# Three changes of order in a fused two-layer transformer on one core: choice of experts, first queries of layer 1, sums of x's quarters

## The chip, the core and the metric

One core of one Trainium2 chip runs the whole program in one launch. The core has five engines that work side by side and meet through semaphores: TensorE (PE, matrix products; its weight loads are listed as PEld), VectorE (DVE), ScalarE (ACT), GpSimd (POOL) and SyncE (SP, which here only issues DMAs). The metric is the device time of one execution in microseconds, lower is better; times are medians of runs. Verdicts on a pair of kernels come with a 95% interval.

## The reference

Eight batches of 512 tokens of 512 features go through two post-norm layers. Layer 0 is causal attention with 16 heads of 32 and a mixture of 8 experts, of which each token takes the best two. Layer 1 is grouped-query attention behind a root-mean-square norm, and a gated network with integer weights. Cut to what the change touches:

```python
x = L0_attn_x                                     # (8, 512, 512)
x = _layernorm(x + _L0_attn_ref(x, ...))          # causal, 16 heads of 32
x = _layernorm(x + _L0_ffn_ref(x, ...))           # 8 experts, top 2
x = _layernorm(x + _L1_attn_ref(x, ...))          # 8 query heads, 2 key/value heads of 64
x = _layernorm(x + _L1_ffn_ref(x, ...))           # silu(gate) * up, hidden 1408

# in _L0_attn_ref
v = (x @ WV_w.T + WV_b).reshape(b, s, NH, HD).transpose(0, 2, 1, 3)
# in _L0_ffn_ref
probs = jax.nn.softmax(router_logits, axis=-1)
routing_weights, selected = jax.lax.top_k(probs, TOP_K)
routing_weights = routing_weights / routing_weights.sum(-1, keepdims=True)
# in _L1_attn_ref
q = (h @ Wq.T).reshape(b, s, H, dh)
k = (h @ Wk.T).reshape(b, s, G, dh)
v = (h @ Wv.T).reshape(b, s, G, dh)
```

## The kernel before

**The stages.** Layer 0's attention runs for the eight batches one after another (from the start to about 670 us), and the choice of experts for each batch runs among the attention of the batches behind it. Then come the experts' tiles (to about 1048 us): rows of 128 tokens are gathered for one expert each, pass its two products, and are written to DRAM. Then layer 1's attention (to about 1580 us) and its integer network (to the end at 2083 us).

**Layer 0's attention.** `attention0` works on one batch `b`, four groups of four heads `g`, and three units `u` of key tiles (`UNITS`). A slot is a pair (g, u). In each slot it issues the scores on PE, their exponential on ACT (L1573) and the causal select on POOL (L1583); then the thunks that `plan` has put into `todo` for that slot; then the product with the values of the unit before; then the thunks of `late`. At u = 1 `normalise` closes the group of heads before: a product sums the rows (rs), ACT and DVE build the inverse (L78 to L81), and DVE multiplies it into the output (L1634). `normed[0]` holds that last instruction. POOL then adds the inverse to a guard's total (L1110). For each unit DVE adds the exponentials up (L1620, "sum of p" below). Products that end in the shared pool of two PSUM banks (`mm`: queries, keys, projections, value products, logits, ranks) need a bank that its last reader has emptied.

**Sums of x's quarters.** From batch 1 on, the value projection is computed with seven products instead of eight (`seven`, order 1, 6, 2, 5, 3, 7, 4). Four of them read sums of quarters of x^T, not x^T itself. `seven_of_rows` (L798, the subtraction at L806) makes these four sums on DVE, 128x512 elements each, from the next batch's x^T, which SP loads while the present batch runs. `plan` puts two of them into `late` of slot (0, 2) and two into slot (1, 0) (for the first batch (2, 1) and (2, 2)). `seven` empties its banks with L1437 on DVE and L1440 on ACT.

**Choice of experts.** `Router.choose(b)` makes from the logits the two best experts of each token, with small DVE instructions on 128x32 and 128x4 elements (L534 to L565). `both` and `earlier` count the tokens that former tiles gave to each expert. `dispatch(b)` multiplies these by two constant matrices (ps_rank, with L564's `earlier` as the second product's input), and so gets each token's place in its expert's list. In a batch b > 1, `choose(b - 2)` stands in slot (0, 0), and slot (1, 0) issues, in this order, the projection of the batch before (ps_o, emptied by L1495 into x), the first of the seven products, and `dispatch(b - 2)`.

**What sets the order.** In `attention0` PE's order is as written at the start and the end (`in_order`); the other engines are ordered by the framework's scheduler, which places instructions by when it expects their inputs. `tc.issue_after(i)` keeps what is issued inside it behind instruction i. From the experts' tiles on, and in layer 1's attention, PE, DVE, ACT and POOL all run in the order written.

**The seam to layer 1.** The first batch of layer 1's attention is prepared beside the last tiles of the experts: `first_pieces` gives a list of steps, of which one is taken after every second tile: fetches, adds, the norm, blocks of a transpose, two empty steps, and then the key, value and first query products, each copied out of PSUM by ACT (L1853, L1862, L1871). Behind the last tile comes a branch that skips three rare tiles (`rare`, L1070, the branch at L1074), in which all engines take part; then layer 1's attention loads ACT's table for the exponential (L1929) and starts with the scores, which read the key and the query.

Of the kernel before, what the change touches and what calls it, by code (L numbers as in the profile page):

```python
# [14 lines left out]
ALU = mybir.AluOpType  # L15
# [421 lines left out]
class Router:  # L437
# [80 lines left out]
    def choose(self, b, parts, ps, columns):  # L518

        nc, small = self.nc, self.small  # L520
        here = slice(NT * b, NT * (b + 1))

        def bc(a):
            return a[:, :, None].to_broadcast([P, NT, E])

        for t in range(NT):
            matmul_by_columns(nc, ps[:, t, :], parts[:, ts(t, P)], self.gather, columns=columns)
        pr = small.tile([P, NT, E], F32, name="pr")
        tmp = small.tile([P, NT, E], F32, name="tmp")
        top = small.tile([P, NT], F32, name="top")  # L530
        second = small.tile([P, NT], F32, name="second")
        red = small.tile([P, NT], F32, name="red")
        total = small.tile([P, NT], F32, name="total")
        nc.vector.tensor_reduce(red, ps, AX.X, ALU.max)  # L534
        nc.vector.tensor_tensor(tmp, ps, bc(red), ALU.subtract)
        nc.scalar.activation(tmp, tmp, AF.Exp)
        nc.vector.tensor_reduce(red, tmp, AX.X, ALU.add)
        nc.vector.reciprocal(red, red)
        nc.vector.tensor_tensor(pr, tmp, bc(red), ALU.mult)

        def first_of_largest(values, largest, one_hot):
            nc.vector.tensor_reduce(largest, values, AX.X, ALU.max)
            nc.vector.tensor_tensor(tmp, values, bc(largest), ALU.is_equal)
            nc.vector.tensor_tensor(tmp, tmp, self.iota, ALU.mult)
            nc.vector.tensor_reduce(red, tmp, AX.X, ALU.min)
            nc.vector.tensor_tensor(one_hot, self.iota, bc(red), ALU.is_equal)

        first_of_largest(pr, top, self.hots[:, 0, here, :])

        rest = small.tile([P, NT, E], F32, name="rest")  # L550
        nc.vector.scalar_tensor_tensor(rest, self.hots[:, 0, here, :], -2.0, pr, ALU.mult, ALU.add)
        first_of_largest(rest, second, self.hots[:, 1, here, :])
        nc.vector.tensor_tensor(total, top, second, ALU.add)
        nc.vector.reciprocal(total, total)
        nc.vector.tensor_tensor(self.weights[:, 0, here], top, total, ALU.mult)
        nc.vector.tensor_tensor(self.weights[:, 1, here], second, total, ALU.mult)


        self.both = small.tile([P, NT, E], F32, name="both")
        nc.vector.tensor_tensor(self.both, self.hots[:, 0, here, :], self.hots[:, 1, here, :], ALU.add)  # L560
        self.earlier = small.tile([P, NT, E], F32, name="earlier")
        nc.vector.tensor_copy(self.earlier[:, 0, :], self.carry)
        for t in range(1, NT):
            nc.vector.tensor_tensor(self.earlier[:, t, :], self.earlier[:, t - 1, :], self.both[:, t - 1, :], ALU.add)  # L564
        nc.vector.tensor_tensor(self.carry, self.earlier[:, NT - 1, :], self.both[:, NT - 1, :], ALU.add)  # L565

    def dispatch(self, b, ps, columns):

# [765 lines left out]
def attention0(env, guard, keep, routes, experts, dram, p_mm, tiles_ctx):  # L1334
# [4 lines left out]
    tc, nc, ins, xs, vec = env.tc, env.nc, env.ins, env.xs, env.vec  # L1339
# [4 lines left out]
    with ExitStack() as phase:  # L1344
# [77 lines left out]
        def row_sums(b):  # L1422
            return seven_of_rows(nc, xts[b], t_x)

        def seven(b, n):
            x_of, _ = row_sums(b)
            room = v_rooms[b % 2]
            ps = mm([P, 2, 256], f"ps_{n}of7")
            for s in range(2):
                for k in range(2):  # L1430
                    matmul_by_columns(nc, ps[:, s, :], x_of[n][:, k, ts(s, P)], v_of[n][:, k, :], start=k == 0, stop=k == 1)

            def block(i, j):
                return room[:, 2 * j : 2 * (j + 1), 256 * i : 256 * (i + 1)]

            def add(out, a):
                nc.vector.tensor_tensor(out, ps, a, ALU.add)  # L1437

            if n == 1:
                nc.scalar.copy(block(0, 0), ps)  # L1440
            elif n == 6:
                add(block(1, 0), block(0, 0))
            elif n == 2:
                add(block(0, 0), block(0, 0))
            elif n == 5:
                add(block(1, 1), block(1, 0))
            elif n == 3:
                add(block(0, 1), block(1, 1))
            elif n == 7:
                add(block(1, 1), block(1, 1))  # L1450
                add(block(1, 0), block(1, 0))
            else:
                add(block(1, 0), block(1, 0))
# [186 lines left out]
        merging, inverses, normed = {}, [], [None]  # L1640
# [6 lines left out]
        def plan(b):  # L1647

            todo, late = ({(g, u): [] for g in range(ND) for u in range(len(UNITS))} for _ in range(2))
            if b == 0:  # L1650
                for slot, places in (((0, 0), (0, 1)), ((0, 1), (3,)), ((0, 2), (2,))):
                    todo[slot] += [lambda t=t: value(b, t) for t in places]
                late[1, 0] += [lambda: v_sums(False), spread_bias]
                todo[1, 1].append(out_of_bias)
                late[1, 1].append(lambda: v_sums(True))
            else:
                todo[0, 0].append(lambda: seven(b, ORDER[-1]))
            pb, last = b - 1, b == NB - 1
            by_dma = 0 <= pb < by_blocks
            for g in range(ND):  # L1660
                nb, ng = (b, g + 1) if g + 1 < ND else (b + 1, 0)
                if nb < NB:
                    todo[g, 0 if by_dma and ng == 0 else 1].append(lambda nb=nb, ng=ng: query(nb, ng))
                    todo[g, 1 if by_dma and ng == 0 else 2].append(lambda nb=nb, ng=ng: key(nb, ng))
            if b:
                places = ((1, 0), (1, 1), (1, 2), (2, 0)) if by_dma else ((1, 0), (1, 0), (1, 1), (1, 1) if last else (1, 2))
                for t, slot in enumerate(places):
                    todo[slot].append(lambda t=t: project(pb, t))
                if by_dma:
                    todo[2, 1].append(lambda: blocks(pb))  # L1670
                else:
                    for c in range(ND):
                        at = todo[2, 1] if last and c >= 2 else (late if last else todo)[2, 0]
                        at.insert(c % 2 if at is todo[2, 1] else len(at), lambda c=c: turn(pb, c))
                todo[(3, 2) if by_dma else (2, 1)].append(lambda: score(pb))
                if not by_dma:
                    todo[(3, 0) if last else (2, 2)].append(lambda: choose(pb))
            if b == 0:
                todo[1, 0].append(lambda: router.merge_lora(mm([P, ND, E], "ps_wr")))
            if b + 1 < NB:  # L1680
                for slot, last_sums in (((0, 2), False), ((1, 0), True)) if b else (((2, 1), False), ((2, 2), True)):
                    late[slot].append(lambda last_sums=last_sums: row_sums(b + 1)[1](last_sums))
                for n, slot in zip(ORDER, ((1, 0), (2, 0), (2, 1), (2, 2), (3, 0), (3, 2)) if b else
                                   ((3, 0), (3, 0), (3, 1), (3, 1), (3, 2), (3, 2))):
                    todo[slot].append(lambda n=n: seven(b + 1, n))
            if b > 1:
                todo[0, 0].append(lambda: choose(b - 2, mm=aside))
                todo[1, 0].append(lambda: dispatch(b - 2))
                if last:
                    todo[1, 2].append(lambda: behind(enter(one_hot(b - 2, range(NT))), normed[0]))  # L1690
                else:
                    todo[1, 2].append(lambda: enter(one_hot(b - 2, range(NT))))
            if last:
                todo[1, 2].append(soon)
                todo[2, 2].append(first_rows)
                late[3, 1].append(first_turned)
                todo[3, 2] += [begin, lambda: dispatch(b - 1)]
            return todo, late
# [96 lines left out]
class Attention1:  # L1795
# [83 lines left out]
    def first_pieces(self):  # L1879
# [7 lines left out]
        def blocks(tiles):  # L1887
            for t in tiles:
# [1 line left out]

        return ([lambda t=t: fetch(t) for t in range(NT)] + [lambda t=t: do["add"](t) for t in range(NT)]
                + [do["deviations"], do["norm"], lambda: blocks((0, 1)), lambda: blocks((2, 3)), lambda: None, lambda: None]
                + [do["key"], do["value"], lambda: do["query"](0)])

    def scale(self, c):

# [554 lines left out]
```

## Time and profile before

| | us |
|---|---|
| median of 3 runs | 2086.05 |
| lowest and highest run | 2085.02, 2086.63 |
| the profiled execution, its own time | 2084.99 |
| its span, first to last instruction | 2083.3 |
| granted clock of PE, mean | 0.998 |

Busy time of PE by stage, from the view by windows (columns: us of the window, then busy us and number of instructions of each engine, the granted clock, the share of the DMA engines and GB/s):

```profile
50.00:150.00 100.00, 100.00 (x1346) 36.73 (x1338) 58.14 (x68) 40.27 (x48) 40.28 (x35) 1.00 0.13 44
...
250.00:350.00 100.00, 100.00 (x1488) 38.29 (x1484) 74.84 (x143) 44.65 (x59) 47.05 (x44) 1.00 0.40 121
...
450.00:550.00 100.00, 98.99 (x1400) 36.74 (x1392) 71.25 (x135) 41.16 (x54) 44.56 (x39) 1.00 0.37 120
...
1000.00:1100.00 100.00, 97.40 (x484) 41.44 (x485) 40.93 (x47) 33.39 (x54) 29.10 (x24) 1.00 0.34 101
```

The second column is PE: it is busy nearly without a break in each window. The fourth is DVE, the sixth POOL. A row of the waits, as the prediction shows them, reads: who waited on which line, for whom, us in total, how often, and the longest. A row of a timeline: start, length, engine, line, operation, what it writes and reads, and in brackets the idle time of the engine before it and who ended it.

### The profile page before, as it was taken

The page shows a single profiled execution, that of the slowest core. Times are in us where ns is not written, and L with a number is a line of the kernel's source. Part 1 is how long each engine was busy: PE and PEld are TensorE (multiplying, and loading weights), DVE is VectorE, ACT ScalarE, POOL GpSimd, SP SyncE. Part 2 cuts the span into 40 slices and gives each one's busy share as a digit, 9 for nine tenths or more (in the row PEclk, how much of TensorE's full clock was granted, in tenths as well). Part 3 has the DMA queues.
Part 4 walks back from the last instruction along what each step waited for, and adds up shares of the span by engine and source line. Part 5 has one row for each costly group of instructions (what it writes and reads, how often), then busy time and mean ns, then how long its engine had stood idle before and what let it go on. Part 6 is the DMA issues. An engine that isn't in the chain of part 4 may idle for free. (4 is left out here: it accounts for less than half of the span.)

```text
span 2083.3 us, 37551 instructions
## 1 busy us (share of the span) xinstructions
PE 2058.4 (99%) x15778; PEld 1069.4 (51%) x15778; DVE 1264.3 (61%) x2047; ACT 645.3 (31%) x916; POOL 510.7 (25%) x509
## 2 busy tenths in 40 slices
PE   9999999999999999999999999999999999999998
PEld 2333333333334677764433333333335888888886
DVE  3667687686777533233158889887868644455444
ACT  2444434344344111111143333333332322222222
POOL 1344444444435121221052231232101000000000
PEclk9999999999999999999999999999999999999999
DMA  6023424415334488876432332223102311111000
GB/s 208 22 83 123 143 81 145 150 63 173 107 139 177 153 222 256 245 228 187 129 102 62 112 122 71 77 96 102 41 1 71 101 41 61 61 61 61 21 21 22
DMA packets 193059, 226.10 MB, mean 109 GB/s; under 512 B 73818, under 2 KB 139610, under 8 KB 189298
## 3 DMA queue, kind: packets, MB, share of 16 engines
q1 hardware_dynamic: 180240, 185.44, 28.3%
q0 software_dynamic: 10560, 34.61, 5.7%
q10 hardware_dynamic: 2082, 3.56, 0.6%
q8 instruction: 127, 2.08, 0.4%
q14 instruction: 50, 0.41, 0.1%
HBM read 138.88 MB, written 84.69 MB: 107 GB/s over the span
## 5 line engine op out<-in xcount | busy, mean ns | idle before, releaser
L1573 ACT ACTIVATE p<-sc 128x2048 f32<-128x2048 f32 (+1 forms) x96 | 152.4, 1587 | 175.8 <-PE sc L67 175.8
L1262 DVE SCALAR_TENSOR_TENSOR hT<-ps_u,vec,sg 128x512 f32<-128x512 f32 x88 | 65.6, 745 | 189.4 <-PE ps_u L1257 189.1
L1583 POOL TENSOR_SCALAR_AFFINE_SELECT p<-p 128x512 f32<-128x512 f32 x128 | 97.2, 771 | 307.6 <-ACT p L1573 302.0
L1273 PE MATMUL ps_f<-ffn_w,h_half 128*128 128x512 f32 x664 | 167.6, 393 | 2.8 <-DVE h_half L1268 2.0
L990 PE MATMUL ps_gu<-xrT,experts 128*128 128x256 f32 x736 | 166.6, 379 | 0.0
L1110 POOL TENSOR_TENSOR g_total<-g_total,r_inv 128x512 f32<-128x512 f32 x64 | 83.7, 1308 | 316.2 <-DVE r_inv L2007 270.6
L1620 DVE TENSOR_TENSOR p<-p 128x1536 f32<-128x1536 f32 (+2 forms) x96 | 147.8, 1539 | 17.7 <-POOL x L1593 10.0
L990 PEld LDWEIGHTS ps_gu<-xrT,experts 128*128 128x128 f32 x736 | 139.3, 190 | 35.9 <-issue 19.3
L1977 ACT ACTIVATE p<-sc 128x1024 f32<-128x1024 f32 x128 | 124.2, 1022 | 100.5 <-PE sc L67 99.2
L2007 DVE RECIPROCAL r_inv<-r_inv 128x512 f32<-128x512 f32 x32 | 107.1, 3347 | 71.6 <-ACT r_inv L1107 71.6
L1273 PEld LDWEIGHTS ps_f<-ffn_w,h_half 128*128 128x128 f32 x664 | 122.9, 188 | 34.5 <-DVE h_half L1268 7.4
L1257 PE MATMUL ps_g<-x_high,ffn_w 128*128 128x512 f32 x352 | 137.2, 390 | 0.0
L1257 PE MATMUL ps_g<-x_low,ffn_w 128*128 128x512 f32 x352 | 137.0, 389 | 0.0
L1257 PE MATMUL ps_u<-x_low,ffn_w 128*128 128x512 f32 x352 | 136.9, 389 | 0.0
L1257 PE MATMUL ps_u<-x_high,ffn_w 128*128 128x512 f32 x352 | 136.9, 389 | 0.0
L67 PE MATMUL ps_q<-experts 128*32 128x512 f32 x1024 | 120.1, 603 | 6.1 <-DMA experts<-in_xT 4.3
L67 PE MATMUL sc<-qT,kT 64*64 64x512 f32 x1024 | 124.7, 602 | 1.2 <-ACT qT L1871 0.9
L1260 ACT ACTIVATE sg<-ps_g,vec 128x512 f32<-128x512 f32 x88 | 60.6, 689 | 195.6 <-PE ps_g L1257 195.6
L1996 PE MATMUL av<-p,v 128*64 128x512 f32 x512 | 120.8, 593 | 0.0
L202 POOL TENSOR_SCALAR rstd<-mv 128x4 f32<-128x4 f32 x15 | 3.9, 262 | 461.9 <-DVE mv L201 461.9
L67 PE MATMUL ps_k<-experts 128*32 128x512 f32 x1024 | 116.4, 595 | 0.0
L67 PE MATMUL ps_o<-attn_out,aoT 128*64 128x512 f32 x512 | 116.4, 598 | 0.0
(310 smaller groups left out, 3419.2 us busy)
## 6 DMA issues: line engine op xcount, KB each, us to landing
results<-y SPq DMA_DIRECT2D x68, 256.0 KB, 2.6
pair<-xrT SPq DMA_DIRECT2D x30, 512.0 KB, 3.3
xrT<-pair SPq DMA_DIRECT2D x120, 128.0 KB, 3.9
turned<-turned SPq DMA_DIRECT2D x56, 256.0 KB, 4.1
merged<-merged SPq DMA_DIRECT2D x48, 256.0 KB, 2.4
experts<-merged SPq DMA_DIRECT2D x8, 1536.0 KB, 6.6
x<-in_x SPq DMA_DIRECT2D x8, 1024.0 KB, 8.4
merged<-in_gate_up SPq DMA_DIRECT2D x32, 256.0 KB, 3.9
```

What stands on the lines that cost most here:

```text
L67: nc.tensor.matmul(out[m], lhsT=lhsT[:, m], rhs=rhs, start=start, stop=stop)
L990: nc.tensor.matmul(ps[:, j, :], lhsT=w, rhs=xT[:, c, :], start=c == 0, stop=c == ND - 1)
L1110: self.nc.gpsimd.tensor_tensor(self.total, self.total, r_inv, ALU.add)
L1257: nc.tensor.matmul(ps, lhsT=w[:, ts(dc, P)], rhs=x[:, dc, :], start=(dc, i) == (0, 0), stop=(dc, i) == (ND - 1, 1))
L1262: nc.vector.scalar_tensor_tensor(hT, u, vec[:, V_SU + c : V_SU + c + 1], sg, ALU.mult, ALU.mult)
L1273: self.nc.tensor.matmul(os[t], lhsT=h[:, ts(t, P)], rhs=self.weights(2 * NHID + c), start=(c, i) == (0, 0), stop=(c, i) == (NHID - 1, 1))
L1573: nc.scalar.activation(p, sc[:, :, :width], AF.Exp, scale=scale)
L1583: select = nc.gpsimd.affine_select(out=first, in_=first, pattern=[[0, 4], [1, P]], compare_op=ALU.is_ge, fill=0.0, base=0, channel_multipl ...
L1620: nc.vector.tensor_tensor(total[:, :, P * kt :], total[:, :, P * kt :], p[:, :, at : at + w], ALU.add)
L1977: nc.scalar.activation(p, sc, AF.Exp, scale=scale)
L1996: nc.tensor.matmul(st["av"][HD * j : HD * (j + 1), :], lhsT=st["v"][:, kt, HD * j : HD * (j + 1)], rhs=p[:, j, :], start=kt == 0, stop=kt ...
L2007: nc.vector.reciprocal(r_inv, r_inv)
```

## The change

Three edits, each of order alone; what is computed stays the same.

1. In `Router.choose`, the four instructions that turn the two best probabilities into weights (sum, reciprocal, two products) are written behind the sums over former tiles, no longer ahead of them.
2. In `Attention1.first_pieces`, the first query product and its copy take the step before the value product and its copy, and the value product the last step.
3. In `attention0`, the sums of x's quarters for the next batch are issued behind `normed[0]`, the instruction that finished the last normalised tile when the sums are issued. The slots stay.

```diff
@@ Router.choose
         first_of_largest(rest, second, self.hots[:, 1, here, :])
-        nc.vector.tensor_tensor(total, top, second, ALU.add)
-        nc.vector.reciprocal(total, total)
-        nc.vector.tensor_tensor(self.weights[:, 0, here], top, total, ALU.mult)
-        nc.vector.tensor_tensor(self.weights[:, 1, here], second, total, ALU.mult)
-
-
         self.both = small.tile([P, NT, E], F32, name="both")
...
         nc.vector.tensor_tensor(self.carry, self.earlier[:, NT - 1, :], self.both[:, NT - 1, :], ALU.add)
+        nc.vector.tensor_tensor(total, top, second, ALU.add)
+        nc.vector.reciprocal(total, total)
+        nc.vector.tensor_tensor(self.weights[:, 0, here], top, total, ALU.mult)
+        nc.vector.tensor_tensor(self.weights[:, 1, here], second, total, ALU.mult)
@@ attention0
         def row_sums(b):
             return seven_of_rows(nc, xts[b], t_x)
+
+        def sums_of_rows(b, last):
+            with tc.issue_after(normed[0].ins):
+                row_sums(b)[1](last)
@@ attention0, plan
                 for slot, last_sums in (((0, 2), False), ((1, 0), True)) if b else (((2, 1), False), ((2, 2), True)):
-                    late[slot].append(lambda last_sums=last_sums: row_sums(b + 1)[1](last_sums))
+                    late[slot].append(lambda last_sums=last_sums: sums_of_rows(b + 1, last_sums))
@@ Attention1.first_pieces
-                + [do["key"], do["value"], lambda: do["query"](0)])
+                + [do["key"], lambda: do["query"](0), do["value"]])
```

In the built program this moves the following. On PE, the first query product (4 instructions) and the value product (16) change places, and the sixteenth value product stands behind the branch. On ACT, the two copies change places. On DVE, the four sums of each of the batches 1 to 6 leave the places where they stood (two ahead of a sum of p, one on either side of the fourth product's emptying) and stand behind L1634, three of them ahead of a sum of p and one after it, in front of L1495; the first batch's four move likewise. POOL and SP keep their order, and the instructions of `choose` keep theirs.

## The prediction

> **What bounds the kernel now.** I read the page first, then the waits of PE over the whole span, the waits of DVE while layer 0's attention runs (100 to 650 us), the form of the one line that the third edit moves, and the timeline of one batch and of the seam between the expert tiles and layer 1's attention.
>
> ```profile
> PE 2058.4 (99%) x15778; PEld 1069.4 (51%) x15778; DVE 1264.3 (61%) x2047; ACT 645.3 (31%) x916; POOL 510.7 (25%) x509
> ```
>
> PE is busy for 2058.4 of 2083.3 us, and the granted clock is 9 tenths or more in every slice. No edit changes a product, so the change can only win back waits of PE, or add some. The waits of PE that bear on the three edits:
>
> ```profile
> engine line waited for: us in total, times, longest us
> ...
> PE ps_q L67 <- DVE experts L1437: 1.4, 2, 1.0
> ...
> PE sc L67 <- ACT qT L1871: 0.9, 1, 0.9
> ...
> PE ps_rank L67 <- DVE earlier L564: 0.7, 1, 0.7
> ```
>
> These three rows are all the change aims at: 3.0 us, or 0.14% of the span. A measurement of this kernel can tell about 0.2%, 4.2 us, from no change. The other engine's view is far larger, and misleads:
>
> ```profile
> DVE experts L806 <- DMA experts<-in_xT: 31.1, 5, 7.2
> ...
> L806 DVE TENSOR_TENSOR experts<-experts x20: 675/692/1802, 171.3 to 511.1; 128x512 f32<-128x512 f32 x20
> ```
>
> L806 holds the sums of x's quarters. Five times DVE stood in front of them until the next batch's x had landed, 31.1 us in all. PE did not stand with it: of that, only what reaches PE counts, and it is the 1.4 us above (the bank of a value product, emptied late by L1437, that the next query product wants).
>
> **First edit, weights behind the sums over former tiles: nothing.** It aims at the 0.7 us of the last row, where the ranks' product waits for L564. But DVE isn't under a written order there. In the built program the small instructions of the choice stand on DVE in the same order before and after, in all eight batches: the scheduler had interleaved them already (in the trace L555 and L556 run between steps of the second choice). Count, durations and waits are the same. This is the case in which the change doesn't do what it says, and for this part it is certain. Cost 0; if the order did change, the bound is 0.7 us gained.
>
> **Second edit, query ahead of value: 0.8 us gained.** At the seam the timeline says:
>
> ```profile
> 1045.66 1.28 ACT L1929 ACT_TABLE_LOAD   x1 [0.45 <-ACTq L1074]
> ...
> 1048.12 0.20 ACT L1929 ACTIVATE p_none<-neg_half 128x1 f32<-128x1 f32 x1 [1.17 <-PEq L1074]
> ...
> 1048.22 0.57 ACT L1871 COPY qT<-ps_q 128x512 f32<-128x512 f32 x1
> ...
> 1048.84 0.21 PEld L67 LDWEIGHTS sc<-qT,kT 64*64 64x64 f32 x8 [1.69 <-ACT qT L1871]
> ```
>
> The query product is the last before the branch that skips the rare tiles. Its copy is queued on ACT behind the table load and an empty exponential that itself waits for PE's side of the branch. Only then may the scores start, at 1048.84. With the query first, its copy falls where the value's copy stood (1036.48, beside expert tiles), and the scores need nothing of ACT. In its place the value's copy goes behind the table load; the first reader of the values (L1996) comes after two pairs of scores and another query product, at 1056.5. The products take as long either way (3.60 us for the query, 3.73 for the values). In the built program one of the 16 value products falls behind the branch (3.73/16 = 0.23 us), ahead of the scores. The score's wait was 0.9 us by the row; its sequencer work behind the branch is done by about 1048.4, so 0.46 us is the floor of the gain. On top, the last product before the branch is a short one (0.27 against 0.59 us), which lets the branch go 0.3 to 0.5 us earlier, less the 0.23. I take 0.8, with ends at 0.4 and 1.0.
>
> The Trainium skill speaks against this step (ScalarE: Activation LUTs, What ACT_TABLE_LOAD costs): a switch of tables costs the load of 1283 ns and a drain of 1380 ns. The trace agrees on the load (1.28), and by the row ACT is held until 1048.12 by the branch. By the rule it would be held to 1045.66 + 2.66 = 1048.32 whatever the branch does; the value's copy would then end by 1049.1 (estimate: 0.20 + 0.57 behind it). The first exponential can't start before the first scores, at about 1049.2 (1050.05 less 0.8). Row and rule give the same sum here, with 0.1 us to spare.
>
> **Third edit, sums behind a normalised tile: 1.4 us gained, 2.3 us lost.** The four sums of a batch leave their places (two before the sums of p, two inside the choice) and stand behind the product of L1634, three before the next sum of p and one after. Six batches have them so (the first batch's four move too, with much room: nothing). Their first reader, the product ps_6of, loads at 303.7 us in the batch shown below, some 25 us on. In the batch at 250 us:
>
> ```profile
> 252.87 1.42 DVE L806 TENSOR_TENSOR experts<-experts 128x512 f32<-128x512 f32 x2 [5.83 <-DMA experts<-in_xT]
> ...
> 254.20 2.96 DVE L1620 TENSOR_TENSOR p<-p 128x1536 f32<-128x1536 f32 x2
> ...
> 262.13 1.80 DVE L806 TENSOR_TENSOR experts<-experts 128x512 f32<-128x512 f32 x1
> ...
> 275.55 0.69 DVE L1634 TENSOR_TENSOR aoT<-av,r_inv 128x512 f32<-128x512 f32 x1
> 275.67 1.28 POOL L1110 TENSOR_TENSOR g_total<-g_total,r_inv 128x512 f32<-128x512 f32 x1 [4.36 <-DVE r_inv L81]
> ...
> 276.16 1.87 DVE L1620 TENSOR_TENSOR p<-p 128x1024 f32<-128x1024 f32 x1
> ```
>
> Gain: without the wait and the two sums, the sum of p at 254.20 starts at 251.1, when its select on POOL ends; without the other two (1.80 + 0.68) the choice ends about 3.5 us earlier. The next sum of p can then start when its select ends, at 268.72 instead of 271.64, and L1634 ends at about 273.4 instead of 276.24: 2.8 us earlier. L1437 empties its bank 2 to 3 us earlier, more than the longest wait of 1.0, so both waits of PE's row go: 1.4 us.
>
> Cost: what is late next is the emptying of the projection's bank, x<-ps_o of L1495. The ranks' product reuses that bank. The same timeline has L1495 end at 277.95 + 0.68 = 278.63 and the first weight load of ps_rank at 279.13: a margin of 0.50 us, and 0.44 to 0.57 in the other four such batches (five batches have ranks and sums both). Now L1634, three sums, the sum of p, one sum and L1495 stand in a row. Bare, four sums cost 4 x 0.69 = 2.76, against 2.8 gained: L1495 ends when it did. But POOL's g_total and two merges (1.28, then 3.51 for two from 276.90) follow the same r_inv, start 2.8 us earlier too, and run beside the three sums.
>
> Here the Trainium skill's rule (SBUF — State Buffer, Who interferes with whom) weighs most: a DVE instruction with two SBUF inputs and a GpSimd instruction that reads SBUF exclude each other, and whichever starts first holds the shared port for its whole length. The sums have two SBUF inputs. The row shows the case: the sum at 262.13, just behind a merge's start, took 1.80 instead of 0.69, 1.11 us lost. By the row alone, 5 of 20 sums were hit, one in four: 0.28 us a sum, about 1.1 a batch as before, no change, and the margin holds: cost 0. By the rule, each of the three sums meets a POOL instruction: 3 x 1.11 = 3.3. The sum of p behind them is freed of its own such wait (1.87 against about 1.22, halfway between the 0.69 of 512 columns and the 1.75 of 1536): 0.65 back. That leaves 2.7 late, less the margin 0.5: 2.2 us a batch, 11 us in five. I take about half of the port waits, 1.6, since the first sum overlaps g_total only in part and the last may come between: 1.6 - 0.65 - 0.5 = 0.45 a batch, 2.3 us in five.
>
> **Sum.** -0.8 - 1.4 + 2.3 = +0.1 us on the profiled execution, whose own time was 2084.99 us (span 2083.3). The median of the runs, 2086.05, lies 1.06 above it, so I put the changed kernel at 2086.2.
>
> **Rivals.**
> - *The ranks' product becomes the new wait.* Place: ps_rank in five batches; price up to 2.2 us each. From (4.2 + 2.2)/5 = 1.3 us a batch it decides. At full price: 2086.05 - 2.2 + 11 = 2094.9. For it: the rule, the 1.80 row, the thin margin. Against: DVE gains 2.8 us before it, and POOL's order may leave gaps. 0.14.
> - *Clean gain.* No port waits reach PE: -2.2, so 2083.8, which still counts as no change. To pass 0.2%, the other DVE waits of PE in this stretch (ps_x1T 0.7, ps_q on x1T 0.3, ps_rank 0.7) must go too, and a little more: 2086.05 - 2.2 - 1.7 = 2082.1 or less. Their order isn't touched. 0.08.
> - *The sums' wait never reached PE*, and the two ps_q waits stay: with the seam alone 2085.2. Part of no change.
>
> No change holds 0.78. The range 2083.3 to 2090.5 runs from a little under the clean gain (2083.8) to a stall of 1.3 us a batch (2090.3).
>
> **What would show it.** Right: DVE's 31.1 us before L806 gone; ps_q's wait on L1437 gone; the scores at the seam start without a wait for ACT; ps_rank waits for x of L1495 in five batches, each under 1 us; sums of 1.1 to 1.8 us beside g_total and the merges. Wrong: ps_rank waits of over 1.3 us, or a PE wait that isn't named here.

## The result, and the profile after

| | before | after |
|---|---|---|
| median of 20 runs each, us | 2085.85 | 2089.05 |
| lowest and highest run | 2084.63, 2086.83 | 2088.06, 2091.31 |
| the profiled execution, its own time | 2084.99 | 2091.31 |
| its span | 2083.3 | 2089.6 |

The ratio is 1.0016, with an interval of 1.0009 to 1.0023: 3.2 us slower, which is within 0.2% and still not nothing. The profiled execution of after is 2.26 us above its median, so its trace holds more than the 3.2 us that have to be explained.

The line of busy times shows no more work on PE than before, and DVE busier by 10.7 us in as many instructions:

```profile
PE 2059.9 (99%) x15778; PEld 1069.3 (51%) x15778; DVE 1275.0 (61%) x2047; ACT 647.2 (31%) x916; POOL 507.7 (24%) x509
```

The waits of PE over the whole span of after (us in total, times, longest):

```profile
PE ps_rank L67 <- DVE x L1497: 4.0, 5, 0.8
PE sc L67 <- ACT qT L1873: 2.9, 1, 2.9
...
PE ps_rank L67 <- DVE earlier L558: 0.7, 1, 0.7
```

The two waits of ps_q for L1437 (L1439 now) are gone. Five waits of the ranks' product for the projection's bank have come (L1497 is the old L1495), and one of 2.9 us in front of scores of layer 1. The last row, which the first edit was to shorten, is unchanged.

The waits of DVE from 100 to 650 us in front of that sum of p, before and after:

```profile
DVE p L1620 <- POOL x L1593: 10.0, 2, 5.3
...
DVE p L1622 <- POOL x L1595: 37.0, 7, 5.3
```

The 31.1 us in front of the sums of quarters have not turned into work done sooner: DVE now stands 37.0 us, not 10.0, in front of the next sum of p, until POOL's add behind the select has ended (L1595; in the batch below the select ends at 251.95, the add at 253.21, and the sum of p starts at 253.24). The prediction had it start when the select ends; PE doesn't feel the difference. An engine that isn't the bottleneck only changed what it waits for.

A wait's row starts when the engine's last instruction is modelled to end, so I also lined the products of the two traces up one by one, and noted where the later one falls back or catches up. Worked out so, steps of over 0.15 us:

```
product of before's trace (us)      step of after (us)
9.55    ps_k, first batch           +0.39   (behind x's first transfer)
180.56  ps_q                        -0.47
197.58  ps_rank                     +0.98
279.34  ps_rank                     +1.01
361.11  ps_rank                     +1.01
442.95  ps_rank                     +0.94
508.78  ps_q                        -1.06
525.80  ps_rank                     +0.99
1048.84 sc, first of layer 1        -0.40   (from the last product ahead of the exchange, 1030.14)
1058.36 sc, second pair             +2.93
end                                  6.29 in all
```

Five ranks' products make +4.93, two query products -1.53, the seam -0.40. That is 3.0 us and agrees with the medians. (The runs' expectations below take 0.3 for the seam: that counts only from the expert tiles behind the exchange, which already run 0.13 us earlier because the query product is that much shorter than the value product.) The 2.93 and the 0.39 are on top of it in this execution.

The timeline of the batch that the prediction looked at, after (start, length, engine):

```profile
273.10 0.69 DVE L1636 TENSOR_TENSOR aoT<-av,r_inv 128x512 f32<-128x512 f32 x1
273.22 1.28 POOL L1108 TENSOR_TENSOR g_total<-g_total,r_inv 128x512 f32<-128x512 f32 x1 [0.69 <-DVE r_inv L81]
...
273.71 4.72 DVE L804 TENSOR_TENSOR experts<-experts 128x512 f32<-128x512 f32 x3
274.45 3.42 POOL L853 TENSOR_TENSOR merged<-merged,scaled 128x512 f32<-128x512 f32 x2
...
277.83 1.09 POOL L1585 TENSOR_SCALAR_AFFINE_SELECT p<-p 128x512 f32<-128x512 f32 x1
278.35 1.65 DVE L1622 TENSOR_TENSOR p<-p 128x1024 f32<-128x1024 f32 x1
...
279.92 0.68 DVE L804 TENSOR_TENSOR experts<-experts 128x512 f32<-128x512 f32 x1
...
280.52 0.68 DVE L1497 TENSOR_TENSOR x<-ps_o,x 128x512 f32<-128x512 f32 x1
...
281.25 0.27 PE L67 MATMUL ps_rank<-both,r_before 128*32 128x32 f32 x8 [0.80 <-DVE x L1497]
```

Three sums take 4.72 us in a row, beside POOL's total and two merges, which take 4.70. Behind them stand the sum of p, the fourth sum and the emptying of ps_o, and PE starts the ranks 0.05 us after that ends. One by one in the trace, DVE and POOL take turns: POOL starts at 273.22, 274.45 and 276.14, the sums at 273.71, 274.97 and 276.66, and the merges are stretched too, to 1.73 and 1.74 us against 1.28 for one at 279.13 us of before. The other four batches read the same to 0.01 us in the three sums (4.71 or 4.72) and 1.65 in the sum of p.

The seam of after:

```profile
1049.39 1.28 ACT L1931 ACT_TABLE_LOAD   x1 [0.45 <-ACTq L1072]
1051.76 0.20 ACT L1931 ACTIVATE p_none<-neg_half 128x1 f32<-128x1 f32 x1 [1.08 <-PEq L1072]
...
1051.92 0.46 PE L67 MATMUL ps_v<-attn_qkv,hT 128*128 128x128 f32 x2 [0.30 <-PEq L1072]
...
1052.31 1.95 PE L67 MATMUL sc<-qT,kT 64*64 64x512 f32 x16
1052.42 0.59 ACT L1864 COPY v<-ps_v 128x512 f32<-128x512 f32 x1 [0.46 <-PE ps_v L67]
...
1064.12 0.58 ACT L1873 COPY qT<-ps_q 128x512 f32<-128x512 f32 x1 [6.07 <-remote]
...
1064.76 1.95 PE L67 MATMUL sc<-qT,kT 64*64 64x512 f32 x16 [2.86 <-ACT qT L1873]
```

The first scores wait for nothing, as meant; two value products stand ahead of them, behind the branch. Further on, the copy of the second pair's queries starts 3.9 us after its product's modelled end, where before it started 0.05 us after.

### The profile page after: what moved, and what is told of

Read it like the earlier page. It is cut to its first block, busy times and chain, and to the rows that moved or that the text cites. A ratio compares the mean times of both kernels' runs of the same rounds, so it can differ in the third digit from the quotient of the medians.

```text
span 2089.6 us, 37552 instructions
## 1 busy us (share of the span) xinstructions
PE 2059.9 (99%) x15778; PEld 1069.3 (51%) x15778; DVE 1275.0 (61%) x2047; ACT 647.2 (31%) x916; POOL 507.7 (24%) x509
## 5 line engine op out<-in xcount | busy, mean ns | idle before, releaser
L67 PE MATMUL ps_q<-hT,attn_qkv 128*64 128x512 f32 (+1 forms) x504 | 116.2, 596 | 0.0
```

Source lines behind the costliest of these rows:

```text
L67: nc.tensor.matmul(out[m], lhsT=lhsT[:, m], rhs=rhs, start=start, stop=stop)
```

## The experiments

Each ran with before beside it: `after_again`, `query_alone`, `sums_alone` and `no_merges` on chip 7, `sums_moved`, `products_earlier`, `sums_and_weights` and `weights_forced` on chip 5, the other four on chip 12. On chip 5 before itself spread from 2084.30 to 2092.20 us. The theory: the whole 3.2 us is the third edit's (sums that stand ahead of the bank's emptying and are stretched by POOL), less a small gain at the seam. The rivals: the second edit brings a lasting wait of 2.9 us; or the number of sums on DVE's queue costs, not POOL beside them.

### The edits taken apart

`after_again` is the changed kernel, unaltered. `query_alone` is before with the second edit, `sums_alone` before with the third.

> The changed kernel once more, unaltered. In its first profile the products stand 6.3 us later at the end than before: five stalls of 0.94 to 1.01 us at the ranks' product (4.93 in all), -1.53 at two query products, -0.32 at the seam, +0.39 in the first 10 us, and +2.93 in front of the second pair's scores of layer 1. Theory (the 2.93 belongs to that one execution): the 2.93 is absent from this profile, the five stalls are there again to 0.05 us each, and the median stays about 3.2 us over before (4.93 - 1.53 - 0.32 = 3.1). Rival (the 2.93 is a lasting wait that the second edit brings): it is there again.

> Before with the second edit alone (layer 1's first queries ahead of its values). Theory: the scores at the seam start 0.3 us earlier against the expert tiles, nothing else moves; time 0.3 us below before (0.9998 or 0.9999). Rival (a wait of 2.9 us in front of the second pair's scores comes with this edit): 2.6 us above before (1.0012). By the prediction on record it would be 0.8 below.

> Before with the third edit alone (the four sums of x's quarters behind the normalised tile). Theory (the third edit makes the whole loss): five stalls of about 0.98 us at the ranks' product, the two waits of the query product for L1437 gone, 4.93 - 1.53 = 3.4 us above before (1.0016). Rival (the second edit makes most of the loss): 0.9 us above (2.3 - 1.4, as the prediction on record has it), 1.0004.

Measured: `sums_alone` 2089.50 us against 2085.61, ratio 1.0018 (1.0009 to 1.0027). Its products step back by 0.98, 1.02, 1.01, 0.93 and 0.98 us at the ranks and forward by 0.47 and 1.08 at ps_q: +3.4, as the theory had it. The third edit alone makes the loss.

`query_alone` was 1.0012 (1.0003 to 1.0021) and `after_again` 1.0032 (1.0019 to 1.0044), and both traces have the wait in front of the second pair's scores (2.90 and 2.91 us). Here the rival was ahead and the theory's "that one execution" was wrong. At the seam the second edit gained 0.40 us in both, counted as in the table above.

### Whose wait is it

`query_again` is `query_alone` at another time and on another chip (12, not 7), beside `before_again`, the kernel before with a second profile.

> The second edit alone, once more, at another time on the chip. If the wait of 2.9 us in front of the second pair's scores belongs to the edit, it is there again and the time is about 2 us over that of before beside it; if it belongs to the time on the chip or to chance, it is absent here, or the kernel before shows one of its kind too, and the two medians lie within 1 us.

> The kernel before, unaltered, with a second profile beside the other three runs: the control for the wait in front of the second pair's scores. If that wait is chance or belongs to the time on the chip, it shows here as in other kernels at times (0 to 2.9 us); if it comes with the second edit alone, it is absent here, as in the first profile of before.

`query_again` 2085.18 us against 2085.76, ratio 1.0000 (0.9991 to 1.0009); `before_again` 1.0001 (0.9992 to 1.0010). The same program without the wait:

```profile
1048.13 0.20 ACT L1929 ACTIVATE p_none<-neg_half 128x1 f32<-128x1 f32 x1 [1.08 <-PEq L1074]
...
1048.68 1.95 PE L67 MATMUL sc<-qT,kT 64*64 64x512 f32 x16
...
1056.60 0.58 ACT L1871 COPY qT<-ps_q 128x512 f32<-128x512 f32 x1 [2.48 <-PE ps_q L67]
...
1058.20 1.95 PE L67 MATMUL sc<-qT,kT 64*64 64x512 f32 x16
```

The copy stands 0.05 us after its product, and all of the trace ends 0.22 us ahead of before's. So the second edit is worth 0.4 us at the seam, too little for its interval, and the wait isn't a necessary part of it. Over all fourteen profiled executions the copy started this long after its product's end, in us:

```
before 0.05   before_again 0.05   query_again 0.05   products_earlier 0.05
sums_merges 0.05   all_kept 0.05   sums_alone 0.91   weights_forced 1.14
sums_and_weights 2.50   sums_moved 2.55   no_merges 3.18
query_alone 3.91   after_again 3.92   after 3.94
```

About 1 us is free, the rest is PE's wait. Two kernels that don't hold the second edit (`sums_moved`, `sums_and_weights`) waited 1.54 and 1.50 us there, four that hold it waited 2.2 to 2.9, and `query_again`, `products_earlier` and `all_kept`, which hold it too, did not. What makes the copy late stays open. In all fourteen traces the copy starts 0.02 us behind an update of PE's semaphore, so what comes late is PE's signal, not ACT; no other instruction, transfer or code fetch in the trace ends there.

Two things go together with the wait, and no run separates them from it. The five traces of chip 12 or of the first profile of before have 0.05 us, and all eight late ones come from chip 7, from chip 5, or from `after`, whose chip isn't on record. The same nine traces (the late ones and `products_earlier`) lack semaphore updates: of the 16 landings of the first gather behind this place they hold 4 to 8, the other five hold all 16. The kernel before has no profile on chip 7 or 5. The times say that the edit counts on chip 7: five of the 11 runs of `query_alone` took 2089.2 us or more, none of the 23 of before beside them over 2088.1. On chip 12, ten of the 11 runs of `query_again` stayed under 2086.6.

### Is it POOL beside the sums

`no_merges` is the changed kernel without POOL's adds of the merged weights.

```diff
-        return {0: load, 1 + i: lambda: nc.gpsimd.tensor_tensor(w[0], w[0], scaled, ALU.add),
+        return {0: load, 1 + i: lambda: None,
```

> The changed kernel without GpSimd's adds of the merged expert weights (they are left out, so the experts use weights without their low-rank part); the running total of the inverses stays. Theory (GpSimd's work beside the sums is what stretches them): the three sums, 4.71 us in a row now, take about 2.6 (three at 0.61 to 0.69 and one wait for the running total), so x of the projection is added 2.1 us earlier, all five waits of the ranks' product go, and the time falls about 4.9 us below the changed kernel, to some 2084 us. Rival (the sums' number on VectorE's queue is what costs, not their neighbours): the three sums stay at about 4.7 us, the waits stay near 0.98 us each, and the time stays near 2089.

The same stretch of the timeline:

```profile
273.16 2.54 DVE L804 TENSOR_TENSOR experts<-experts 128x512 f32<-128x512 f32 x3
275.62 1.21 DVE L1622 TENSOR_TENSOR p<-p 128x1024 f32<-128x1024 f32 x1
...
278.25 0.69 DVE L1497 TENSOR_TENSOR x<-ps_o,x 128x512 f32<-128x512 f32 x1 [0.37 <-PE ps_o L67]
...
279.72 0.24 PE L67 MATMUL ps_rank<-both,r_before 128*32 128x32 f32 x8
```

The order on DVE is the same, the three sums take 2.54 instead of 4.72, the sum of p 1.21 instead of 1.65, L1497 now waits for the product that fills its bank, and the five waits of the ranks are gone. The rival of the queue's length falls. The time didn't follow: 1.0030 (1.0018 to 1.0042). Without the adds other waits came, for a reason that wasn't looked into: 2.43 us of steps at 349 to 350 us with this row among them:

```profile
PE sc L67 <- DMA lora<-in_lora: 1.2, 1, 1.2
```

and 2.17 us again at the second pair. So the run shows the mechanism, not its worth.

### The merges moved away from the sums

`sums_merges` is the third edit with the merges queued behind the select of their unit. Nothing is left out; the rows of PE, DVE and ACT are those of `sums_alone`.

```diff
-            with behind_return() if g == 3 and u else ExitStack():
+            with behind_return() if g == 3 and u else ExitStack(), tc.issue_after(select.ins):
                 for thunk in merging.pop(n, []):
```

> The third edit alone, with GpSimd's merges queued behind the select of their unit, so that they no longer run beside the sums; nothing is left out, and the rows of TensorE, VectorE and ScalarE are those of the third edit alone. Theory (the stretching by GpSimd's work is what makes the sums late): the three sums take about 2.5 us in a row instead of 4.7, all five stalls of the ranks' product (4.93 us in all) are gone, the 1.53 us of the two query products stay gained, so the products end about 1.5 us ahead of before's if the seam is quiet. Rival (the merges stretch something else as much where they stand now, the sums of p or the one-hot tiles): a new wait of 0.5 us or more in each of the five batches, and no gain over before.

```profile
268.73 1.27 POOL L855 TENSOR_TENSOR merged<-merged,scaled 128x512 f32<-128x512 f32 x1
268.78 1.27 DVE L546 TENSOR_TENSOR r_hots<-r_iota,red 128x32 f32<-128x32 f32 x1
...
275.96 2.54 DVE L806 TENSOR_TENSOR experts<-experts 128x512 f32<-128x512 f32 x3
...
278.43 1.65 DVE L1624 TENSOR_TENSOR p<-p 128x1024 f32<-128x1024 f32 x1
278.97 2.25 POOL L855 TENSOR_TENSOR merged<-merged,scaled 128x512 f32<-128x512 f32 x1
280.00 1.77 DVE L806 TENSOR_TENSOR experts<-experts 128x512 f32<-128x512 f32 x1
281.69 0.68 DVE L1499 TENSOR_TENSOR x<-ps_o,x 128x512 f32<-128x512 f32 x1
```

The three sums fell to 2.54 us, as the theory said, and the kernel was slower all the same: 1.0033 (1.0021 to 1.0045), steps of 1.39 to 1.49 us at the ranks, 7.15 in all. The rival won. One merge now runs beside the choice, where an instruction of 32 columns takes 1.27 us instead of 0.19, and the other beside the fourth sum, 1.77 instead of 0.68. Both are ahead of the emptying of the bank, in a row that has no other gap.

### The sums moved behind the emptying of the bank

`sums_moved` holds the third edit only, with the four sums behind the x<-ps_o of the projection.

```diff
-            with tc.issue_after(normed[0].ins):
+            with tc.issue_after((added[0] or normed[0]).ins):
                 row_sums(b)[1](last)
...
-            nc.vector.tensor_tensor(xs[b][:, t, :], ps, xs[b][:, t, :], ALU.add)
+            added[0] = nc.vector.tensor_tensor(xs[b][:, t, :], ps, xs[b][:, t, :], ALU.add)
...
-                for slot, last_sums in (((0, 2), False), ((1, 0), True)) if b else (((2, 1), False), ((2, 2), True)):
+                for slot, last_sums in (((1, 0), False), ((1, 0), True)) if b else (((2, 1), False), ((2, 2), True)):
```

> Before with the four sums queued behind x<-ps_o of the projection instead of behind the normalised tile (no other edit). Theory (the sums only cost because they stand ahead of the emptying of the projection's bank): all five stalls of the ranks' product are gone, the two waits of the query product for L1437 stay gone, the sums still stretch beside GpSimd's merges, and the time is 1.5 us below before (0.9993), 4.9 below the third edit alone. Rival (any place behind the normalised tile delays the ranks, through what follows on VectorE): ranks' results and the one-hot tiles come up to 4 us later and new waits of TensorE take up the gain, no faster than before.

```profile
277.81 0.69 DVE L1499 TENSOR_TENSOR x<-ps_o,x 128x512 f32<-128x512 f32 x1 [3.20 <-PE ps_o L67]
278.42 1.89 DVE L806 TENSOR_TENSOR experts<-experts 128x512 f32<-128x512 f32 x3
...
288.28 0.75 DVE L1481 TENSOR_SCALAR q<-ps_q,vec 128x512 f32<-128x512 f32 x1
...
289.08 1.07 PE L1631 MATMUL rs<-p,ones 128*32 128x512 f32 x8
```

The five stalls are gone, the query products keep their gain (0.47 and 1.08), and the sums run bare: three in 1.89 us, which gives the cost of POOL beside them as 4.72 - 1.89 = 2.83. But DVE's row from the ranks on, one small instruction behind another, has no gap either, and the emptying of ps_q comes later; the row sums' product waits for it in five batches (steps of 0.28 to 0.34). That gives 1.6 us back, all of the 1.5, and the wait at the second pair (1.54) stood in this execution too: 0.9999 (0.9990 to 1.0008). The interval holds the theory's 0.9993 as well; it is the steps that decide. The theory had the stalls right, the rival the end.

### The first edit, done by force

The built order of DVE is the same with the first edit as before. `weights_forced` queues the weights behind the carry; `sums_and_weights` does so on top of `sums_moved`.

```diff
-        nc.vector.tensor_tensor(self.carry, self.earlier[:, NT - 1, :], self.both[:, NT - 1, :], ALU.add)
+        carried = nc.vector.tensor_tensor(self.carry, self.earlier[:, NT - 1, :], self.both[:, NT - 1, :], ALU.add)
+        with self.env.tc.issue_after(carried.ins):
             nc.vector.tensor_tensor(total, top, second, ALU.add)
```

> Before with the weights alone forced behind the sums over former tiles. Theory: the one wait of 0.98 us at the last batch's ranks' product shrinks by 0.3 to 0.6 us and nothing else moves by over 0.3 us. Rival (the order of these small instructions is worth nothing, as the built program's unchanged order under the change makes it look): no step at that product.

> The sums behind x<-ps_o, and the weights forced behind the sums over former tiles by an order on VectorE's queue (which the change as it stands does not do). Theory: as with the sums alone moved (1.5 us below before), and at the last batch the wait of the ranks' product for the sums over former tiles, 0.98 us, shrinks by 0.3 to 0.6 us: 1.9 below before (0.9991). Rival (VectorE's gaps held the weights for nothing, so taking them out gains nothing): the 0.98 us stays.

```profile
PE ps_rank L67 <- DVE earlier L560: 0.7, 1, 0.7
```

A miss: the row is that of both traces, PE's wait for `earlier` stayed at 0.7 us, with no step at that product, and `sums_and_weights` came to 1.0002 (0.9993 to 1.0011); `weights_forced` is one execution. The weights did move: in before's trace they run at 714.11 to 714.78 us, in the gaps of a chain of dependent instructions, and in `weights_forced` behind the last of the sums over former tiles. So the first edit would be worth nothing even where it moved something. What does lie between those sums in both traces is three DVE instructions of the experts' first tiles, 0.68 to 0.71 us each against 0.12 to 0.19 for a sum (in before `h` at 715.03, `xrT` at 715.71 and 716.38). No run moved them.

### The seam without a product across the branch

`products_earlier` is `query_alone` with one empty slot less, so that key, query and value come two tiles sooner; `all_kept` puts that together with `sums_merges`.

```diff
-                + [do["deviations"], do["norm"], lambda: blocks((0, 1)), lambda: blocks((2, 3)), lambda: None, lambda: None]
+                + [do["deviations"], do["norm"], lambda: blocks((0, 1)), lambda: blocks((2, 3)), lambda: None]
```

> Before with the second edit, and one empty slot of the list taken out, so that key, query and value each stand two expert tiles earlier and the last product ahead of the branch is an expert's. Theory (the 2.9 us in front of the second pair's scores comes from the value product lying across the branch, two of its products behind it): that wait is absent, the two products behind the branch (0.46 us) are gone too, and the time is about 0.8 us below before. Rival (it comes from the query's copy standing early, wherever the value's stands): the wait of 2.9 us is there again, about 2.5 us above before. A second rival: the tiles of x wanted by the key's product are not ready two tiles earlier, and a new wait stands in front of ps_k.

> The sums and merges as in the run beside this one, and key, query and value two expert tiles earlier. Theory: as the sums and merges alone, and no wait in front of the second pair's scores; 1.5 us below before. Rival: the seam's wait of 1.5 to 2.9 us comes whatever stands across the branch, and the gain is gone.

```profile
1050.35 1.95 PE L67 MATMUL sc<-qT,kT 64*64 64x512 f32 x16 [0.90 <-ACTq L1074]
1050.56 1.28 ACT L1929 ACT_TABLE_LOAD   x1 [0.45 <-ACTq L1074]
1051.85 0.20 ACT L1929 ACTIVATE p_none<-neg_half 128x1 f32<-128x1 f32 x1
1051.96 1.92 ACT L1977 ACTIVATE p<-sc 128x1024 f32<-128x1024 f32 x2
```

The wait at the second pair was absent in both, but the trace shows nothing gained; the time, 0.9995 (0.9986 to 1.0004) for `products_earlier`, can't tell it from the theory's 0.9996. With no product left to cover it, PE waits 0.90 us for ACT's side of the branch, and the first exponential then waits for the table, so that the second scores wait 0.73 us instead of 0.33. `all_kept` was 1.0034 (1.0022 to 1.0047), the ranks' stalls of `sums_merges`.

No version here beats before by what its interval can tell.

## Why the prediction was right, and where it was off

The forecast was no change within 0.2%, at 2086.2 us. It held, and the 2089.05 lies inside the range of 2083.3 to 2090.5; but the middle was 2.85 us too low, and the sign of the small change, which it left open, is slower. That it held owes much to the width of that band, 4.2 us: the prediction's own sum was -0.8 - 1.4 + 2.3 = +0.1, the runs' is -0.40 - 1.53 + 4.93 = +3.0. In part that was luck.

- **First edit, nothing**: right, and for the reason given. Its bound of 0.7 us was too generous; `weights_forced` shows none of it.
- **Second edit, 0.8 gained**: the mechanism was right, the size was twice too large. The five traces that hold the edit in this form (`after`, `after_again`, `query_alone`, `query_again`, `no_merges`) show 0.40 each, the low end that was given. Two terms were mis-sized. The first is "the last product before the branch is a short one ... which lets the branch go 0.3 to 0.5 us earlier, less the 0.23". Against the last product ahead of the exchange, 3.87 us later in after than in before, ACT was released 0.23 us earlier (1048.12 before, 1051.76 after), and 0.13 of that is the shorter query product in the value product's place. Behind the release two value products stand, not one. From it to the scores it is 0.72 us before (1048.12 to 1048.84) and 0.55 after (1051.76 to 1052.31): 0.17 gained. The second is the wait. With its floor of 0.46 the terms make 0.53 to 0.73, so the 0.8 also counted on a part of the row's 0.9 us above the floor. No more than the floor came: 0.46 for the wait, 0.23 for the branch and -0.29 for the two value products give the 0.40. The rule on the table's drain, weighed there, is not borne out: in `products_earlier` the next instruction of ACT starts at 1051.85, where the load ends. In before's trace the loads at 709.18 and 1576.84 us start 0.02 us behind the instruction ahead of them, and the next starts 0.01 us behind them.
- **Third edit, gain of 1.4**: right. Both waits went, 1.53 by the steps.
- **Third edit, loss of 2.3**: place and mechanism were right (x<-ps_o of L1495, five batches, under 1 us by the waits' row), the size is 4.93. The mis-sized term is "I take about half of the port waits, 1.6 ... 0.45 a batch". Measured in the batch shown: the sums lost 2.83 to POOL, not 1.6; the sum of p won back 0.22 (1.87 to 1.65), not 0.65, and the next select runs beside it. In DVE's favour L1634 ended 3.35 us earlier against PE, not 2.8: 3.10 ahead of the ranks' product before (279.34 - 276.24), 6.45 after (281.25 - 1.01 - 273.79). From its end to the bank's it took 2.39 before (276.24 to 278.63) and 7.41 after (273.79 to 281.20): 5.02 longer, less 3.35, less the slack of the product, 0.66 (0.71 before, 0.05 after), is 1.01, the step of this batch. The rule as the prediction put it, every sum meets POOL (3.3), was much nearer than the average over the 20 sums of before (one in four). That average came from another place, where POOL was mostly idle.
- **The rivals**: the ranks' product did become the new wait, at 0.94 to 1.01 us a batch, short of the 1.3 from which it was to decide. The clean gain fell with it. That the sums' wait never reached PE fell too.
- **A PE wait that isn't named** was listed as what would make the prediction wrong. There is one, 2.93 us at the second pair of layer 1, in the profiled execution. It comes and goes with the second edit in place, and two kernels without that edit have it too (1.54 and 1.50 us); the two profiles of before do not.

## What to carry to other kernels

Before moving work into a gap of an engine, see what the other engine on the shared port runs in that gap; here the stretch found elsewhere for the same instruction was no guide. Moving the other engine's work did not remove the stretch: in `sums_merges` it came back at the next two-input instructions ahead of the same bank. And waiting time of an engine that isn't the bound is not a budget: of 31.1 us that DVE no longer waits here, PE got 1.5 and paid 4.9.

## What the hardware showed that was not expected

- POOL holds small DVE instructions as long as large ones. In `sums_merges` 128x32 elements took 1.27 us beside a merge of 1.27, against 0.19: 1.08 lost, where the 128x512 sum at 262.13 us of before lost 1.11.
- The same copy behind the same product started 0.05 or up to 3.9 us late in different executions of programs that differ little or not at all. `query_alone` and `query_again` are one program, on two chips; their medians differ by 2.6 us, while those of before beside them differ by 0.15. A single profile of such a spot, or one chip, proves nothing about the change.
